# Attention kernel: one score product split in 128 and 384 columns in half of the phases, and 160 wait instructions a batch between projection products

## Chip, cores, metric

The kernel runs on one core of one Trainium2 chip. The metric is device time in microseconds of one execution, the median of three runs. An engine is named as in the profile: PE is TensorE's matmuls, PEld its weight loads, DVE is VectorE, ACT is ScalarE, POOL is GpSimd, SP is SyncE.

## What is computed

The input x is (32, 256, 32, 32) in f32: 32 batches, 256 channels, 1024 tokens. Each group of 8 channels is normalised over its 8 x 1024 values. From the result q, k and v are projected (256 to 256 each), there are 8 heads of 32 channels, and a strictly causal attention over the 1024 tokens follows; x is added.

```python
x = x + conv_attention(_gn(x), q_w, q_b, kv_w, kv_b)
# in it, by head:
scores = einsum('bhqd,bhkd->bhqk', q, k) / sqrt(32)
scores = where(mask == 0, -10000.0, scores)      # mask: tril(ones, -1)
attn   = where(mask == 0, 0.0, softmax(scores))
out    = einsum('bhqk,bhkd->bhqd', attn, v)
```

## The kernel before

All is f32. A batch is worked through in two halves, one for each group g of four heads (128 channels). Each half has six phases, numbered i = 0 to 5, the entries of the list VISITS; so there are twelve phases a batch, v = 0 to 11, and 32 x 12 in all. The text calls a phase by its i.

**A phase** has four steps on TensorE, and the main loop at the end of `unshifted` writes them down in this order by hand; nothing is reordered later, since the whole body stands in a manual schedule.

1. `scores(b, v)`: the transposed scores of one or two blocks of keys against their queries, as products of 32 rows (a head's channels) by 64 columns of keys. Each entry of VISITS is made once for each of four heads and two halves of the keys. "Long" entries are up to 512 queries wide; their results go into two tiles, `pairs[0]` for heads 0, 1 and `pairs[1]` for heads 2, 3. "Short" entries, among them the diagonal pairs (built by `pair`: one product of 128 and one of 64 columns for each half of the keys), go into `pairs[2]`.[...]
2. the units that fall due at this phase (`at`): one unit of projection for a later phase or batch. `projections(b)` makes twelve of them, `project_qk` eight times (two input halves cc, each four products of 512 columns by `product`, L169) and `project_v` four times (four groups of four products of 256 columns).
3. `values(b, v - 1)`: exponentials of the phase ahead times v (L422), 12 or 16 products.
4. what stands in `between` and `after`: the small products of the norm of a later batch (pm, pv, L169), sums, and the transfers.

ScalarE takes the exponentials of each phase out of PSUM, `pairs[0]`, `pairs[1]` (L397) and then `pairs[2]` (L393), and evicts projections and values. GpSimd masks the diagonals (L339) and issues the adding transfers of key sums, VectorE adds exponentials over keys for the softmax sums and finishes outputs, SP issues loads and stores.

**The order inside `scores`.** It starts with the short entries of heads 2, 3 (`short_of((2, 3))`), then the long ones of heads 0, 1 (`begin`), then the first long one of heads 2, 3. Then TensorE waits until the short entries of heads 2, 3 are finished (semaphore `bank_free`[...]), and the short ones of heads 0, 1 follow. Phases 0, 1, 3 and 4 are in PAIRS, which tells that their short entry is a diagonal pair. Where such a phase has a second long entry (phase 0 alone), its product of heads 0, 1 is put between the two parts of the diagonal pair of heads 2, 3, which then run in reverse order, 64 columns first. Phases 1, 3 and 4 have one long entry, 512 columns wide.

`live["arrived"]` is a semaphore that ScalarE raises to 1 when the first part of x has come, at the very start, and to 2 a little later. SP waits on it in two places; so does GpSimd, 64 times in a row, ahead of its first work (L669).

Of the kernel before, what the change touches and what calls it, by code (L numbers as in the profile page):

```python
# [17 lines left out]
P = 128  # L18
HD = 32
CPG = 8  # L20
HALF = 512
# [11 lines left out]
def tile_norm_attention_residual(  # L33
# [19 lines left out]
    nc = tc.nc  # L53
    B, C, H, W = x.shape
    S = H * W
    NG = C // P
# [42 lines left out]
    def unshifted():  # L99
        live = {}  # L100
# [56 lines left out]
        def spare(name):  # L157

            live["turn"] = live.get("turn", -1) + 1
            if live["turn"] in (1, 3, 5):  # L160
                return ps_o.tile([P, HALF], F32, tag="acc", name=name)
            return misc(name)
# [68 lines left out]
        def norm_apply(b, hf, g):  # L231
# [5 lines left out]
            for s in range(2):  # L237
# [5 lines left out]
                else:  # L243
                    nc.scalar.activation(to, of, AF.Identity, bias=live["shift", b][:, g : g + 1], scale=rstd)  # L244

        def project_qk(b, g, n, hf):

            key = ("qk"[n], b, g)
            if hf == 0:
                live[key] = qkpool.tile([P, S], F32, tag="qk"[n], name=f"{'qk'[n]}_{b}_{g}")  # L250
            cols = slice(hf * HALF, (hf + 1) * HALF)
            pp = spare(f"pp_{b}_{g}_{n}_{hf}")
            for cc in range(NG):
                product(
                    pp, wT[:, cc, n * C + g * P : n * C + (g + 1) * P], live["xn", b, hf][:, cc, :],
                    start=cc == 0, stop=cc == NG - 1,
                )
            nc.scalar.activation(
                live[key][:, cols], pp, AF.Identity, bias=qk_bias[:, n, g : g + 1], scale=(SCALE, 1.0)[n],
            )  # L260

        def project_v(b, n):


            if n == 0:
                live["v", b] = work.tile([P, NB, C], F32, tag="v", name=f"v_{b}")
            pp = spare(f"ppv_{b}_{n}").rearrange("p (s c) -> p s c", c=C)
            hf, at = divmod(2 * n * P, HALF)
            for s in range(2):
                tokens = slice(at + s * P, at + (s + 1) * P)  # L270
                for cc in range(NG):
                    product(
                        pp[:, s, :], live["xn", b, hf][:, cc, tokens], wT[:, cc, 2 * C : 3 * C], start=cc == 0, stop=cc == NG - 1,
                    )
            nc.scalar.copy(live["v", b][:, 2 * n : 2 * n + 2, :], pp)  # L275

        def projections(b):
# [29 lines left out]
        def score(b, g, bank, j, op):  # L307

            c, kb, first, width, cols = op
            rows = slice(HD * j, HD * (j + 1))  # L310
            return nc.tensor.matmul(  # L311
                bank[c : c + KEYS, cols], lhsT=live["k", b, g][rows, kb * P + c : kb * P + c + KEYS],
                rhs=live["q", b, g][rows, first : first + width], start=True, stop=True, skip_group_check=True,
            )

        def scores_of(b, g, bank_of, heads, entries, between=lambda: None, order=slice(None)):
# [9 lines left out]
                                done.setdefault((j, c), []).append(score(b, g, bank_of(j), j, ops[n]))  # L326
            return done

        def mask(b, g, raw, j):


            hf, place = j // 2, (2 * j % 4) * P
            if ("e", b, g, "D", hf) not in live:
                live["e", b, g, "D", hf] = epool.tile(
                    [P, 4, HALF], F32, tag=("e0", "e")[hf], bufs=4, name=f"diagonal_{b}_{g}_{hf}"
                )
            square = live["e", b, g, "D", hf]
            for s in range(2):
                nc.gpsimd.affine_select(  # L339
                    out=square[:, :, place + s * P : place + (s + 1) * P],  # L340
                    in_=raw[:, :, (1 - s) * KEYS : (3 - s) * KEYS],
                    pattern=[[0, 4], [(1, -1)[s], P]], compare_op=ALU.is_gt, fill=0.0, base=0,
                    channel_multiplier=(-1, 1)[s],
                )
            if j == 0:
                nc.gpsimd.memset(square[0:1, :, 0:1], 1.0)

        def scores(b, v):


            g, i = divmod(v, len(VISITS))
            longs, shorts = VISITS[i]
            name = f"{b}_{g}_{i}"
            e = epool.tile([P, 4, HALF], F32, tag="e0" if i == TOTAL else "e", bufs=4, name=f"e_{name}")
            eh = epool.tile([P, 4, HALFBANK], F32, tag="eh", bufs=3, name=f"eh_{name}")
            pairs = [ps_s.tile([P, 2, HALF], F32, tag="sT", name=f"sT_{name}_{a}") for a in range(3)]
            short = pairs[2].rearrange("p bank (n q) -> p bank n q", n=2)
            short_of = lambda heads, *how: scores_of(
                b, g, lambda j: short[:, j % 2, j // 2, :], heads, shorts, *how
            )  # L360
            long_of = lambda heads, n: scores_of(b, g, lambda j: pairs[j // 2][:, j % 2, :], heads, longs[n : n + 1])
            rest = [lambda: long_of((2, 3), 1)] if len(longs) > 1 else []
            begin = [lambda n=n: long_of((0, 1), n) for n in range(len(longs) - 1, -1, -1)]
            if i in PAIRS and len(longs) > 1:
                first = short_of((2, 3), begin.pop(0), slice(None, None, -1))
            else:
                first = short_of((2, 3))
            for f in begin:
                f()
            long_of((2, 3), 0)  # L370

            ends = [made[-1] for made in first.values()]
            first = [ins for made in first.values() for ins in made]
            for ins in ends:
                ins.then_inc(bank_free, 1)
            for ins in first:
                tc.no_tile_sem_insts.add(ins.ins.name)
            live["free"] = live.get("free", 0) + len(ends)
            wait = nc.tensor.wait_ge(bank_free, live["free"])
            for ins in first:  # L380
                tc.declare_no_dep(wait.ins, ins.ins, reason="the semaphore orders them")
            made = short_of((0, 1), *rest if i in PAIRS else ())
            if i not in PAIRS:
                for f in rest:
                    f()
            for made in made.values():
                for lo in made:
                    for ins in first:
                        tc.declare_no_dep(lo.ins, ins.ins, reason="the semaphore orders them")
            wide, narrow = (max(at + width for at, width, _ in entries) for entries in (longs, shorts))  # L390
            for a in range(3):
                if a == 2:
                    exp = nc.scalar.activation(  # L393
                        eh.rearrange("p (n bank) q -> p bank n q", n=2)[:, :, :, :narrow], short[:, :, :, :narrow], AF.Exp
                    )
                else:
                    nc.scalar.activation(e[:, 2 * a : 2 * a + 2, :wide], pairs[a][:, :, :wide], AF.Exp)  # L397

            for ins in first:
                tc.add_to_no_dep_group(f"first_{name}", ins.ins)  # L400
                tc.add_to_no_dep_group("first", ins.ins)
            tc.declare_no_dep(exp.ins, group=f"first_{name}", reason="through the last two products")
            tc.declare_fence(exp.ins, group=f"first_{name}")
            live["e", b, g, "L", i], live["e", b, g, "H", i] = e, eh
            if i in PAIRS:
                mask(b, g, eh, PAIRS[i])

# [182 lines left out]
        ]  # L590
        N, TOTAL = NG * len(VISITS), 2
        PAIRS = {0: 0, 1: 1, 3: 3, 4: 2}

        PRODUCTS = [
            (0, [
# [36 lines left out]
        at, between, after = {}, {}, {}  # L632
# [22 lines left out]
        SPREAD = (2, 2, 4, 5)  # L655
        FINISH = (N + 13, N + 13, N + 14, N + 16)
        every = range(4)
        ALIGN = 24, 64

        with tc.manual_schedule(engines={ENG.PE, ENG.Activation, ENG.DVE, ENG.Pool, ENG.SP}):  # L660
# [4 lines left out]
            load_weights(junk)  # L665
            for _ in range(ALIGN[0]):
                nc.vector.drain()
            for _ in range(ALIGN[1]):
                nc.gpsimd.wait_ge(live["arrived"], 1)  # L669
# [36 lines left out]
            for b in range(B):  # L706
                first, last = b * N, b == B - 1
# [3 lines left out]
                if b >= 2:  # L711
                    for n in range(NG * NH):
                        cols = slice(n % NH * HALF, (n % NH + 1) * HALF)
                        v = max(first - 2 * N + LOAD, 0)
# [4 lines left out]
                if not last:  # L719
                    for n in every:  # L720
                        v = first + SUMS[n]
# [5 lines left out]
                    v = first + N + (5 if late else 6)  # L727
# [8 lines left out]
                    for n in every:  # L736
                        v = first + (N + 9 + n // 2 if late else FINISH[n])
# [12 lines left out]
            for i in range(B * N + 1):  # L750
# [4 lines left out]
                b, v = divmod(i - 1, N)  # L755
# [23 lines left out]
    def shifted():  # L779


        with ExitStack() as inner:
# [34 lines left out]
            with tc.For_i(0, B, 1) as b:  # L817
# [93 lines left out]
                )  # L911

    inside = unshifted()
    ALL = 3 * P * ROW
    held = nc.values_load(
# [29 lines left out]
```

## Time and profile before

| what | value |
|---|---|
| median of three runs | 1793.78 us (1793.7 to 1794.42) |
| the profiled execution | 1793.44 us, its span 1791.7 us |
| mean granted TensorE clock | 0.999 |
| one batch, first projection to first projection | 55.09 us |
| products of the program on TensorE; matmuls in the profile | 18,568; 37,036 |
| TensorE busy at scores, values, q/k projections, v projections | 578.4, 401.0 and 158.7, 492.2, 247.5 us |

How to read it: a matmul of f32 runs as two passes, so the profile has two matmuls and two weight loads for one product of the program. [...]the distance between the starts of groups of four is what a group takes. The ends of matmuls are modelled. Where a text gives starts in ns, they are those of single instructions in the trace, counted from the first score product of the phase.

### The profile page before, as it was taken

What the parts mean: (1) busy time and instruction counts of PE and PEld (TensorE: products, weight loads), DVE (VectorE), ACT (ScalarE), POOL (GpSimd) and SP (SyncE); (2) the same over time, 40 slices, a digit from 0 to 9 for tenths busy, and PEclk for the clock granted to TensorE, in tenths of its full rate; (3) what the DMA queues carried; (4) which work ended last, traced back from release to release, by engine and by line L of the source; (5) the groups of instructions that cost most, each with busy time, mean ns of one, the idle gap of its engine ahead of it and who ended that gap; (6) DMA issues with size and microseconds to landing.
All of it is one profiled execution on the core that took longest, in us unless ns stands there. A gap on an engine that the chain in (4) does not pass through costs nothing.

```text
span 1791.7 us, 81825 instructions
## 1 busy us (share of the span) xinstructions
PE 1784.4 (100%) x37036; PEld 948.2 (53%) x37036; DVE 1673.4 (93%) x1826; ACT 1456.4 (81%) x1990; POOL 881.3 (49%) x903
## 2 busy tenths in 40 slices
PE   9999999999999999999999999999999999999998
PEld 5555555555555555555555555555555555555554
DVE  4689999999999999999999999999999999999998
ACT  6888878888788888788887888878888878888785
POOL 2345544554545555445554455454555544555452
PEclk9999999999999999999999999999999999999999
DMA  2566766767667766766676676767776667666664
GB/s 70 105 115 137 134 134 129 147 135 143 127 126 149 140 138 134 135 139 138 139 135 131 129 150 132 145 125 128 149 141 135 136 134 138 139 139 137 132 107 106
DMA packets 86818, 236.77 MB, mean 132 GB/s; under 512 B 21312, under 2 KB 22336, under 8 KB 70592
## 3 DMA queue, kind: packets, MB, share of 16 engines
q0 software_dynamic: 15872, 97.53, 40.1%
q1 hardware_dynamic: 70448, 133.89, 25.5%
q8 instruction: 290, 4.75, 1.1%
q14 instruction: 64, 0.52, 0.1%
q10 hardware_dynamic: 144, 0.07, 0.0%
HBM read 66.85 MB, written 34.57 MB: 57 GB/s over the span
## 4 chain that ended last, share of the span: by engine, by line
PE 99%; ACT 0%; DVE 0%; issue 0%; POOL 0%; POOLq 0%
PE sT L311 31%; PE acc L422 28%; PE pp L169 26%; PE ppv L169 13%; PE pd L474 1%; PE busy L155 0%; ACT e L397 0%; PE pv L169 0%; PE pm L169 0%; PE wt L148 0%; DVE rb_last L547 0%; ACT eh L393 0%; DVE rb_last L534 0%; DVE turned L531 0%; DVE acc L544 0%
## 5 line engine op out<-in xcount | busy, mean ns | idle before, releaser
L339 POOL TENSOR_SCALAR_AFFINE_SELECT diagonal<-eh 128x512 f32<-128x512 f32 x512 | 632.5, 1256 | 841.5 <-ACT eh L393 840.9
L397 ACT ACTIVATE e<-sT 128x1024 f32<-128x1024 f32 x768 | 744.4, 1022 | 250.3 <-PE sT L311 225.9
L440 DVE TENSOR_TENSOR e<-e,e 128x1024 f32<-128x1024 f32 x314 | 574.2, 1829 | 24.5 <-ACT v L275 3.2
L311 PE MATMUL sT<-q,k 32*64 32x128 f32 (+2 forms) x18432 | 578.4, 372 | 0.1
L311 PEld LDWEIGHTS sT<-q,k 32*64 32x64 f32 x18432 | 394.8, 131 | 188.4 <-PE sT L311 69.6
L169 PE MATMUL pp<-xn,wT 128*32 128x512 f32 x4096 | 492.2, 598 | 0.0
L422 PE MATMUL acc<-e,v 128*32 128x512 f32 (+3 forms) x4608 | 401.0, 450 | 0.0
L393 ACT ACTIVATE eh<-sT 128x768 f32<-128x768 f32 (+1 forms) x384 | 341.7, 890 | 0.0
L422 PEld LDWEIGHTS acc<-e,v 128*32 128x32 f32 x4608 | 149.2, 110 | 261.5 <-issue 238.9
L169 PE MATMUL ppv<-wT,xn 128*32 128x256 f32 x4096 | 247.5, 382 | 0.0
L440 DVE TENSOR_TENSOR diagonal<-diagonal,e 128x1536 f32<-128x1536 f32 x126 | 195.0, 1548 | 16.8 <-PE acc L422 9.2
L169 PEld LDWEIGHTS pp<-xn,wT 128*32 128x32 f32 x4096 | 107.0, 109 | 195.7 <-issue 163.7
L440 DVE TENSOR_TENSOR e<-e,eh 128x1024 f32<-128x1024 f32 x126 | 164.2, 1303 | 6.5
L422 PEld LDWEIGHTS acc<-diagonal,v 128*32 128x32 f32 x4096 | 121.1, 110 | 87.6 <-issue 76.0
L440 DVE TENSOR_TENSOR e<-e,diagonal 128x2048 f32<-128x2048 f32 x63 | 144.2, 2289 | 19.8 <-POOL diagonal L339 19.8
L169 PEld LDWEIGHTS ppv<-wT,xn 128*32 128x32 f32 x4096 | 120.1, 109 | 79.7 <-issue 7.0
L422 PE MATMUL acc<-diagonal,v 128*32 128x128 f32 x4096 | 158.7, 273 | 0.0
L244 ACT ACTIVATE xn<-x,shift,rstd 128x256 f32<-128x256 f32 x248 | 136.8, 608 | 0.6 <-POOL shift L229 0.6
L544 DVE TENSOR_TENSOR num<-num,rb 128x512 f32<-128x512 f32 x124 | 123.3, 994 | 0.2 <-DMA rb<-inverses 0.2
L453 POOL DMA_DIRECT2D e<-e x124 | 103.3, 833 | 38.2 <-issue 38.2
L547 DVE SCALAR_TENSOR_TENSOR rb<-num,v_bias_col,x 128x256 f32<-128x256 f32 x248 | 117.5, 515 | 4.4
L453 POOL DMA_DIRECT2D diagonal<-diagonal x124 | 104.1, 839 | 4.8 <-issue 4.8
(84 smaller groups left out, 984.4 us busy)
## 6 DMA issues: line engine op xcount, KB each, us to landing
x<-in_x_dram SPq DMA_DIRECT2D x124, 256.0 KB, 3.7
diagonal<-diagonal POOLq DMA_DIRECT2D x62, 512.0 KB, 5.4
e<-e POOLq DMA_DIRECT2D x62, 512.0 KB, 5.9
rb<-inverses SPq DMA_DIRECT2D x124, 256.0 KB, 3.9
out_dram<-rb SPq DMA_DIRECT2D x124, 256.0 KB, 4.9
diagonal<-diagonal POOLq DMA_DIRECT2D x62, 256.0 KB, 4.6
folded<-diagonal SPq DMA_DIRECT2D x62, 256.0 KB, 5.1
e<-e POOLq DMA_DIRECT2D x62, 256.0 KB, 5.0
```

What stands on the lines that cost most here:

```text
L169: nc.tensor.matmul(out[part], lhsT=lhsT[:, part], rhs=rhs, start=start, stop=stop, skip_group_check=True)
L244: nc.scalar.activation(to, of, AF.Identity, bias=live["shift", b][:, g : g + 1], scale=rstd)
L311: return nc.tensor.matmul(bank[c : c + KEYS, cols], lhsT=live["k", b, g][rows, kb * P + c : kb * P + c + KEYS], rhs=live["q", b, g][rows, ...
L339: nc.gpsimd.affine_select(out=square[:, :, place + s * P : place + (s + 1) * P], in_=raw[:, :, (1 - s) * KEYS : (3 - s) * KEYS], pattern=[ ...
L393: exp = nc.scalar.activation(eh.rearrange("p (n bank) q -> p bank n q", n=2)[:, :, :, :narrow], short[:, :, :, :narrow], AF.Exp)
L397: nc.scalar.activation(e[:, 2 * a : 2 * a + 2, :wide], pairs[a][:, :, :wide], AF.Exp)
L422: nc.tensor.matmul(acc[HD * j : HD * (j + 1), of], lhsT=live["v", b][:, kb, h * HD : (h + 1) * HD], rhs=e[:, j, :], start=first, stop=last ...
L440: nc.vector.tensor_add(to, to, tile_of(b, g, at))
L453: nc.gpsimd.dma_start(out=total[:rows], in_=total[rows : 2 * rows], accum_op=ALU.add)
L474: nc.tensor.matmul(pd[HD * j : HD * (j + 1), of], lhsT=pick, rhs=e[:, j, :], start=start, stop=stop, skip_group_check=True,)
L544: nc.vector.tensor_mul(num, num, rb)
L547: nc.vector.scalar_tensor_tensor(blocks(rb, s), blocks(num, s, (start + s) % 2 == 1), v_bias_col[:, g : g + 1], blocks(xt[:, g, cols], s), ...
```

## The change

- `part_of` is new: it issues the one long entry of a phase for heads 0, 1 and for a slice of its columns. In `scores`, for the phases in SPLIT (v = 1, 3, 4, 7, 9, 10, which are i = 1, 3, 4 of both halves of a batch), `begin` becomes two pieces, the first 128 columns and the other 384. Since `begin` now has two pieces there, these phases also take the branch that only phase 0 took: the 64-column parts of the diagonal pair of heads 2, 3 come first, then the 128-column piece of heads 0, 1, then the 128-column parts of heads 2, 3, then the 384-column piece. The long product of heads 2, 3 stays whole.
- `fill` is new: n times TensorE waits for `arrived` to be at least 1. It is called after each group of four products of the projections, with the counts in FILL: 14 and 12 in a `project_qk`, 8, 8, 6, 6 in a `project_v`. In the built program two such waits share one instruction: 5120 wait instructions are added, 160 a batch, and 768 products.

```diff
+        def fill(n):
+
+            for _ in range(n):
+                nc.tensor.wait_ge(live["arrived"], 1)
+
         def project_qk(b, g, n, hf):
...
                     start=cc == 0, stop=cc == NG - 1,
                 )
+                fill(FILL[0][cc])
...
                         pp[:, s, :], live["xn", b, hf][:, cc, tokens], wT[:, cc, 2 * C : 3 * C], start=cc == 0, stop=cc == NG - 1,
                     )
+                    fill(FILL[1][NG * s + cc])
...
+        def part_of(b, g, bank, entry, of):
+
+            at, _, halves = entry
+            for j in (0, 1):
+                for ((c, kb, first, _, cols),) in halves:
+                    score(b, g, bank[:, j, :], j, (
+                        c, kb, first + of.start, of.stop - of.start, slice(cols.start + of.start, cols.start + of.stop)
+                    ))
...
             begin = [lambda n=n: long_of((0, 1), n) for n in range(len(longs) - 1, -1, -1)]
-            if i in PAIRS and len(longs) > 1:
+            if v in SPLIT:
+                begin = [lambda n=n: part_of(b, g, pairs[0], longs[0], n) for n in (slice(0, P), slice(P, HALF))]
+            if i in PAIRS and len(begin) > 1:
                 first = short_of((2, 3), begin.pop(0), slice(None, None, -1))
...
         PAIRS = {0: 0, 1: 1, 3: 3, 4: 2}
+        SPLIT = 1, 3, 4, 7, 9, 10
...
         every = range(4)
+        FILL = (14, 12), (8, 8, 6, 6)
         ALIGN = 24, 64
```

## The prediction

> **What bounds the kernel now.** I read the page first: the busy table, then the chain that ended last.
>
> ```profile
> PE 1784.4 (100%) x37036; PEld 948.2 (53%) x37036; DVE 1673.4 (93%) x1826; ACT 1456.4 (81%) x1990; POOL 881.3 (49%) x903
> ...
> PE 99%; ACT 0%; DVE 0%; issue 0%; POOL 0%; POOLq 0%
> PE sT L311 31%; PE acc L422 28%; PE pp L169 26%; PE ppv L169 13%; PE pd L474 1%; PE busy L155 0%; ACT e L397 0%; PE pv L169 0%; PE pm L169 0%; PE wt L148 0%; DVE rb_last L547 0%; ACT eh L393 0%; DVE rb_last L534 0%; DVE turned L531 0%; DVE acc L544 0%
> ```
>
> TensorE is never without work, and the chain is its own: scores (L311), values (L422), projections (L169). A saving counts in full, as long as no other engine comes late. Then the chain in order of time:
>
> ```profile
> 98.32 1.88 PE pp L169 x16
> 125.82 1.89 PE ppv L169 x32
> 153.41 1.88 PE pp L169 x16
> ```
>
> The same projection comes 55.09 us later (153.41 - 98.32): one batch, and it repeats so for all of them. Last, the six phases of the first half of a batch, each as a window from its first score product to the next projection (phases 0, 1, 2, 3, 4, and 5 of the half ahead; columns: window, length, busy time and instructions of PE and PEld at L311, clock, share of the DMA engines, GB/s):
>
> ```profile
> 431.97:433.39 1.42, 1.42 (x64) 1.16 (x64) 1.00 0.51 185
> 436.54:437.94 1.40, 1.40 (x48) 1.06 (x48) 1.00 0.09 18
> 441.10:442.57 1.47, 1.47 (x32) 0.80 (x32) 1.00 0.90 89
> 445.30:446.70 1.40, 1.40 (x48) 1.05 (x48) 1.00 0.96 152
> 450.29:451.69 1.40, 1.40 (x48) 1.05 (x48) 1.00 0.02 1
> 427.34:428.82 1.48, 1.48 (x48) 1.03 (x48) 1.00 0.66 230
> ```
>
> Phases 1, 3, 4 take 1.40 us (single starts: 1404 ns; it is 1403 to 1411 in all batches). Phase 0, which already has a long product of heads 0, 1 in 128 and 384 columns, takes 1.42 (1419 ns). So splitting as such is no gain; the order inside a phase must be followed.
>
> [...] Here it is 91 to 94 ns from the end of the last score column to the first projection.
>
> **The split.** Starts in ns from the start of the phase, the first of each group of four (heads x key halves), both passes:
>
> ```
> phase 0 now   heads 2,3: 64 @0,106    128 @165,276  384 @386,708   128 @1031,1140
>               heads 0,1: 128 @26,186  384 @296,618  128 @941,1050   64 @1159,1215   next @1419
> phase 1 now   heads 2,3: 128 @0,160   64 @269,325   512 @383,815
>               heads 0,1: 512 @53,534  128 @963,1073  64 @1182,1238                  next @1404
> ```
>
> The two head pairs are two chains side by side, and the longer one sets the end. In phase 1 it is that of heads 0, 1: it begins 53 ns late and then has no gap. After the change, phases 1, 3, 4 issue 64 (2,3), 128 (0,1), 128 (2,3), 384 (0,1), 512 (2,3), then 128 and 64 (0,1). That is phase 0's order in the first five groups, with 512 for 384, and without its last 128 of heads 2, 3. So I take phase 0's starts:
>
> - heads 0, 1: 128 @26,186; 384 @296,618; 128 @941,1050; 64 @1159,1215. The fourth of the last group starts 20 later, at 1235, and its columns end at 1235 + 53 = 1288.
> - heads 2, 3: 64 @0,106; 128 @165,276; 512 @386. In phase 0 the second to fourth product of this group load their weights at 355, 371, 388 and not beside the first, at 278. These are products 18 to 20 of the phase; 355 is 32 ns after the first product's end (323)[...]. The changed phase has as many ahead of them, so the delay stays: the fourth streams from 388 + 53 = 441, its second pass from 870, and ends at 870 + 429 = 1299.
>
> The later end is 1299; with 93 for the drain the projection starts at 1392. Now it is 1403.5: 11.5 ns a phase less. Six phases a batch, 32 batches: 192 x 11.5 = **2.2 us less**. Entering a phase costs the same (202 ns after a 128-column value product in phase 0 as in phase 3).[...]
>
> Bounds: without the delayed loads heads 0, 1 decide, 1288 + 93 = 1381, 22.5 less, -4.3 us. If the end is ragged as in phase 0 (1419), 15.5 more, +3.0 us.
>
> **The waits.** fill asks for 14 + 12 in each of eight q/k units and 28 in each of four v units, 320 a batch; the built program has two conditions in one instruction, so 160 instructions a batch, 5120 in all. They stand on TensorE's own queue; behind them are the products of the same unit, then the values. "arrived" is at 1 from the start, so none blocks. What they take is issue time, e each. The only rows:
>
> ```profile
> L169 PEldq EVENT_SEMAPHORE  x67: 51/51/51, 7.2 to 1693.0; - x67
> ```
> ```profile
> L669 POOLq EVENT_SEMAPHORE  x32: 42/43/43, 4.3 to 7.0; - x32
> ```
>
> TensorE's own are 51 ns each, and the products around them keep their 429 ns, so they are taken ahead of the array. GpSimd's 32, in a row and of the same kind, lie 87 ns apart (2.7 us / 31). I take 51 and keep 87 as the upper end. Does issue fall behind? In a changed phase the first projection products have entered by about 1170 (products 12 to 15 end at 1099 to 1119, plus 32 and four times 16.5, the pace of the late loads). A v unit then needs 14 waits and three more groups of 66 ns: the values enter at 1170 + 14e + 198. TensorE asks for them at 1392 + 240 + 7 x 216 = 3144. At e = 51 that is 2082, 1.06 us early; at 87, 2586; it is late only above e = 127. A q/k unit: 1170 + 13e + 66 against 1392 + 453 + 3 x 429 = 3132, late above 145. So the waits cost 0, hidden by the products of their own unit. Before the first scores, TensorE waits for xn and evictions anyway, and 7 waits (357 ns) lie beside 858 ns of products; 0.
>
> **Instruction fetch.** Queue 8 brings TensorE's instructions: 4.75 MB in 290 packets, one for 256 of 74,150 instructions. A batch has 2306 now, nine packets; then 2306 + 24 x 4 + 160 = 2562, ten. No phase differs between batches although the packets' places shift by 2 instructions a batch, so a packet costs nothing now; I take 0.
>
> **Others.** ScalarE's first exponential of a phase starts 1208 ns in, and 1185 in phase 0, so about 23 ns earlier; heads 2, 3 end up to 55 later, but their exponential waits behind the first (1022 ns). Ahead of phase 3 ScalarE's last one ends only 162 ns ahead of the next phase; it moves along with TensorE. No DMA is added or moved; SP's wait for bank_free is met at the same time (128's end at 276 + 268 = 544, now 64's end at 325 + 217 = 542).
>
> Sum: 0 - 2.2 + 0. The profiled execution took 1793.44 (span 1791.7, 1.7 around it), so 1791.2; the median of the runs is 0.34 above it: **1791.6 us**.
>
> **The rivals.**
> - The forecast, 1791.6 (1790.3 to 1793.0). Chance 0.52.
> - The loads are not late[...]: -4.3, 1789.5. For it: phase 1 now shows no late load. Against: the same 16 products are ahead. 0.20.
> - The end is ragged as in phase 0, +3.0: 1796.8. For it: phase 0 measures 1419. Against: its last products are late behind a 128 of heads 2, 3 that the changed phases lack. 0.12.
> - Slower by the waits: with two conditions a wait takes longer than 51. From e = 127 on the values of v units come late. At 131 (1.5 x 87) it is 14 x 131 + 1368 - 3144 = 58 ns in each of 128 units, 7.4 us: 1793.8 - 2.2 + 7.4 = 1799.0. For it: no such instruction is on this queue now. Against: 87 on GpSimd. 0.09.
> - Ten packets in the time of nine: one a batch comes 0.2 us too late, +6.4, 1798.0. Against: issue is over a microsecond ahead. 0.07.
> - That the change does not do what it says is excluded: the built program has 18,568 + 768 products and the 5120 waits.
>
> **How the numbers follow.** About 0.2% (3.6 us) can be told from no change. Forecast, ragged end and a little of the second rival are inside it, 0.62; faster 0.20, the second rival; slower 0.18, the last two and a ragged end that is somewhat worse. The range takes in the first three cases (0.84): 1788.5 to 1797.5.
>
> **What would show it.** Right: phases 1, 3, 4 at about 1392 ns, batches at 55.09 - 0.07 = 55.02 us, late loads at 355 to 388 for the 512 of heads 2, 3, phases 0, 2, 5 as now, projections with 429 and 216 ns between groups. Wrong: gaps in front of values or inside projections (waits), phases that differ from batch to batch (fetch), or 1381 or 1419 for the changed phases.

## The result and the profile after

| | us, median | runs |
|---|---|---|
| before | 1793.74 | 1793.43 to 1794.42 |
| after | 1853.72 | 1844.38 to 1860.76 |

The ratio is 1.0332, with a 95% interval of 1.0298 to 1.0367: 60 us slower, where 2 us faster was forecast. The runs of the kernel after also lie 16 us apart, those of before 1 us. The profiled execution took 1856.89 us, its span 1855.1.

From the page of the kernel after, the busy table and the chain that ended last:

```profile
PE 1809.7 (98%) x38572; PEld 968.1 (52%) x38572; DVE 1655.7 (89%) x1826; ACT 1453.9 (78%) x1990; POOL 817.7 (44%) x903
...
PE 97%; issue 2%; ACT 1%; DVE 0%; DMA 0%; POOLq 0%; POOL 0%; SPq 0%; ACTq 0%
PE sT L318 30%; PE acc L440 28%; PE pp L169 26%; PE ppv L169 13%; PE pd L492 1%; ACT e L415 0%; DMA x<-in_x_dram 0%; PE pm L169 0%; ACT eh L411 0%; PE pv L169 0%; PE wt L148 0%; ACT v L282 0%; POOLq L689 0%; DVE rb_last L565 0%; DVE rb_last L552 0%
```

TensorE is still its own chain, but 2% of the span is "issue": time in which it waited for nothing that the profile shows. That was 0% before. The six phases as windows of the scores (L318), in batch 7 (columns as before: window, length, busy time and instructions of PE and PEld, clock, DMA share, GB/s), phases 0 to 5:

```profile
414.12:415.54 1.42, 1.42 (x64) 1.16 (x64) 1.00 0.98 190
418.69:420.08 1.39, 1.39 (x56) 1.09 (x56) 1.00 0.02 6
423.23:424.71 1.48, 1.48 (x32) 0.80 (x32) 1.00 0.30 33
427.43:428.82 1.39, 1.39 (x56) 1.09 (x56) 1.00 0.96 183
432.68:434.06 1.38, 1.38 (x56) 1.09 (x56) 1.00 0.04 12
437.26:438.74 1.48, 1.48 (x48) 1.02 (x48) 1.00 0.80 282
```

The scores are shorter, as forecast: 1387 to 1388 ns in phases 1, 3, 4 by single starts. So the loss is elsewhere. The view of waits, TensorE's issue rows (us in total, times, longest), before and then after:

```profile
PEld acc L422 <- issue: 315.0, 1144, 0.4
...
PEld ppv L169 <- issue: 7.0, 34, 0.3
```
```profile
PEld acc L440 <- issue: 347.9, 1147, 2.7
...
PEld ppv L169 <- issue: 14.3, 39, 2.6
```

In before a weight load idles ahead of values 1144 times, with the products themselves busy for 1784.4 of the span's 1791.7 us, but never for more than 0.4 us. Now there are idle times of 2.7 us. The same view for the products themselves, where before has no row of issue:

```profile
PE acc L440 <- issue: 26.3, 22, 2.3
PE ppv L169 <- issue: 5.1, 4, 2.1
...
PE sT L318 <- issue: 2.4, 5, 1.2
```

Next I took the distance between the first score products of consecutive phases, less the same distance in before (where it is equal in all batches), over batches 1 to 30, by phase of the batch v (0 to 11). An ordinary table, worked out from the starts in the trace:

```
v             0     1    2     3     4    5    6    7    8     9    10   11    sum
excess, us  0.0   7.3  0.0  24.7  -0.6  0.0  0.3  0.5  0.0  30.3  -0.2  0.0   62.3
```

Three phases hold it all, and not in each batch: one v = 9 loses 4.2 us, another none. The batch, always 55.09 us before, now takes between 54.98 and 60.58. There are 46 places where a product starts over 150 ns later than it should; they sum to 45.7 us, and the rest of the 62 is made of smaller delays in the groups right behind them. **36 of the 46, with 42.7 us, begin at one and the same kind of place**: the executed TensorE instruction number 256k + 449 (counted from 0), which is the first one of packet k of the instruction queue (322 packets for the 82,345 TensorE instructions in the trace, one for 256). The queues on the pages of before and after (packets, MB, share of 16 engines):

```profile
q0 software_dynamic: 15872, 97.53, 40.1%
q1 hardware_dynamic: 70448, 133.89, 25.5%
q8 instruction: 290, 4.75, 1.1%
```
```profile
q0 software_dynamic: 15872, 97.53, 37.3%
q1 hardware_dynamic: 70448, 133.89, 25.5%
q8 instruction: 322, 5.28, 1.2%
```

Here is one such stall, v = 3 of batch 3, in the timeline of the kernel after (start, us, engine, line):

```profile
230.92 1.47 PE L440 MATMUL acc<-e,v 128*32 128x512 f32 x14
233.82 0.38 PE L440 MATMUL acc<-e,v 128*32 128x256 f32 x1 [1.43 <-issue]
```
```profile
231.78 0.12 PEld L440 LDWEIGHTS acc<-e,v 128*32 128x32 f32 x3 [0.30 <-issue]
233.82 0.11 PEld L440 LDWEIGHTS acc<-e,v 128*32 128x32 f32 x1 [1.92 <-issue]
```

Fourteen passes of a group of sixteen run, three of four weight loads, and then nothing for 1.43 us, in the middle of a group whose inputs are all there. The matmul at 233.82 is the first instruction of packet 38. TensorE reached packet 37 at 226.82; the fetch of 38 began only at 231.11 and landed at 232.35; TensorE went on 1.47 us later. The windows around it, after and then in the variant "light_adds" below (columns: window, length, busy of PE, PEld, DVE, ACT, POOL, clock, DMA share, GB/s):

```profile
224.00:228.00 4.00, 4.00 (x92) 1.80 (x81) 3.86 (x7) 4.00 (x7) 1.85 (x3) 1.00 0.82 175
228.00:232.00 4.00, 4.00 (x100) 2.33 (x90) 3.79 (x7) 4.00 (x8) 0.27 (x1) 1.00 0.91 177
232.00:236.00 4.00, 2.57 (x70) 1.38 (x65) 4.00 (x3) 1.15 (x4) 2.93 (x2) 1.00 0.25 74
```
```profile
224.00:228.00 4.00, 4.00 (x112) 2.58 (x108) 3.83 (x8) 3.70 (x6) 0.00 (x0) 1.00 0.35 95
228.00:232.00 4.00, 4.00 (x96) 2.16 (x92) 3.86 (x5) 3.12 (x6) 2.78 (x2) 1.00 0.24 45
```

The packet is late while the DMA engines are 82% and 91% busy. At 35% (light_adds) packet 38 begins 0.39 us after TensorE reached packet 37, not 4.3. The trace of before shows the same relation: where the DMA engines were over 90% busy in the 1.5 us after TensorE reached the packet ahead (118 packets), the fetch began a median of 1.8 us after that moment; where they were under 10% busy (41 packets), it began right at it. Over the whole runs ("slack" is from the landing of a packet to the start of its first instruction on TensorE; "begin" is from TensorE reaching the packet ahead to the beginning of the fetch):

```
                slack, ns                      begin, us         a packet's 256
            min    median   below 1600     median    max         take, median us
before     1604    4334     0 of 277        0.67     3.93        6.04
after      1214    2924    62 of 309        1.30     5.35        5.34
```

In after, all 37 packets at whose first instruction TensorE had started nothing for over 0.3 us have a slack of 1.2 to 1.6 us, so that is how soon it resumes after a landing. Before, the least was 1604: no stall, and nothing to spare.

### The profile page after: what moved, and what is told of

The parts are those of the page before. It is cut to its first block, busy times and chain, and to the rows that moved or that the text cites. A ratio compares the mean times of both kernels' runs of the same rounds, so it can differ in the third digit from the quotient of the medians.

```text
span 1855.1 us, 90017 instructions
## 1 busy us (share of the span) xinstructions
PE 1809.7 (98%) x38572; PEld 968.1 (52%) x38572; DVE 1655.7 (89%) x1826; ACT 1453.9 (78%) x1990; POOL 817.7 (44%) x903
## 4 chain that ended last, share of the span: by engine, by line
PE 97%; issue 2%; ACT 1%; DVE 0%; DMA 0%; POOLq 0%; POOL 0%; SPq 0%; ACTq 0%
PE sT L318 30%; PE acc L440 28%; PE pp L169 26%; PE ppv L169 13%; PE pd L492 1%; ACT e L415 0%; DMA x<-in_x_dram 0%; PE pm L169 0%; ACT eh L411 0%; PE pv L169 0%; PE wt L148 0%; ACT v L282 0%; POOLq L689 0%; DVE rb_last L565 0%; DVE rb_last L552 0%
## 5 line engine op out<-in xcount | busy, mean ns | idle before, releaser
L355 POOL TENSOR_SCALAR_AFFINE_SELECT diagonal<-eh 128x512 f32<-128x512 f32 x512 | 548.2, 1091 | 969.1 <-ACT eh L411 969.1
L318 PE MATMUL sT<-q,k 32*64 32x128 f32 (+2 forms) x19968 | 581.0, 357 | 2.8 <-issue 2.4
L458 DVE TENSOR_TENSOR e<-e,e 128x1024 f32<-128x1024 f32 x314 | 551.8, 1757 | 31.9 <-PE acc L440 7.5
L318 PEld LDWEIGHTS sT<-q,k 32*64 32x64 f32 x19968 | 402.2, 131 | 183.6 <-PE sT L318 61.5
L440 PE MATMUL acc<-e,v 128*32 128x512 f32 (+3 forms) x4608 | 417.5, 454 | 27.7 <-issue 25.1
L440 PEld LDWEIGHTS acc<-e,v 128*32 128x32 f32 x4608 | 153.4, 110 | 297.6 <-issue 270.4
L458 DVE TENSOR_TENSOR e<-e,eh 128x1024 f32<-128x1024 f32 x126 | 170.3, 1352 | 6.5
L565 DVE SCALAR_TENSOR_TENSOR rb<-num,v_bias_col,x 128x256 f32<-128x256 f32 x248 | 123.8, 539 | 4.4
L562 DVE TENSOR_TENSOR num<-num,rb 128x512 f32<-128x512 f32 x124 | 117.8, 950 | 0.1
L458 DVE TENSOR_TENSOR e<-e 128x512 f32<-128x512 f32 x64 | 52.7, 824 | 67.8 <-PE acc L440 58.8
```

The lines of the kernel that those rows point to most:

```text
L318: return nc.tensor.matmul(bank[c : c + KEYS, cols], lhsT=live["k", b, g][rows, kb * P + c : kb * P + c + KEYS], rhs=live["q", b, g][rows, ...
L355: nc.gpsimd.affine_select(out=square[:, :, place + s * P : place + (s + 1) * P], in_=raw[:, :, (1 - s) * KEYS : (3 - s) * KEYS], pattern=[ ...
L440: nc.tensor.matmul(acc[HD * j : HD * (j + 1), of], lhsT=live["v", b][:, kb, h * HD : (h + 1) * HD], rhs=e[:, j, :], start=first, stop=last ...
L458: nc.vector.tensor_add(to, to, tile_of(b, g, at))
L562: nc.vector.tensor_mul(num, num, rb)
L565: nc.vector.scalar_tensor_tensor(blocks(rb, s), blocks(num, s, (start + s) % 2 == 1), v_bias_col[:, g : g + 1], blocks(xt[:, g, cols], s), ...
```

## Experiments

The theory: one packet is fetched ahead (in before a fetch begins from 1.5 us before to 3.9 us after TensorE reaches the packet ahead of it, in after from 0.9 before to 5.35 after, first and last 60 us left out); with more instructions a batch, and instructions that take issue time, the fetches at the DMA-loaded places come too late (theory "fetch"). The rivals: the waits themselves hold TensorE back ("issue"), or the order of the scores does it ("split"). The forecasts ahead of the runs name theories by letters: W and I say that the issue time of the waits does it; P and N, that the number and the place of the packets do, whatever fills them; L, that packets land late because the DMA engines are busy. Each run was made beside runs of the kernel before on the same chip, 1793.4 to 1793.7 us; ratios are to those.

**split_only**: the split, no waits (2402 TensorE instructions a batch; after has 2562, before 2306).

```diff
-        FILL = (14, 12), (8, 8, 6, 6)
+        FILL = (0, 0), (0, 0, 0, 0)
```

> The split with no wait instruction (FILL all 0): 2402 instructions a batch, so the places of the instruction packets drift by 98 a batch. Theory W (the waits: 106 ns of issue each hold TensorE's queue back, so that packets are asked for late and no lead is left to hide one that comes late): no stalls, the split's 16.5 ns in 192 phases alone, 1793.7 - 3.2 = 1790.5 us. Theory P (more than nine packets a batch, at places where a short block meets busy DMA engines, stall, whatever fills them): stalls in those batches in which a packet falls on such a place, 1796 to 1815 us.

Measured: 1800.82 us, 1.0038 (1.0026 to 1.0051). The changed phases take 1387 ns as in after. But v = 10 loses 4.2 us and v = 1 loses 3.9 in the profiled run; 8 of its 12 gaps are at packet starts, and its least slack is 1211 ns. So the split gains, and even its 96 instructions a batch (2402 is no multiple of 256, so packets drift over all places) give back more than the gain.

**waits_only**: the waits, no split (2466 a batch).

```diff
-        SPLIT = 1, 3, 4, 7, 9, 10
+        SPLIT = ()
```

> The waits with no split (SPLIT empty): 2466 instructions a batch. Theory W: stalls at about the rate of the full change, 1835 to 1860 us, issue idle in front of single products all along. Theory P: drifting places, stalls in some batches only, 1800 to 1825 us. If waits alone cost by their issue time and not through packets, gaps come in every unit of v at the same place, and the time is the same in every batch.

Measured: 1827.72 us, 1.0189 (1.0151 to 1.0227), between the two forecasts. The excess (31.1 us) is spread over v = 0, 1, 3, 5, 9 and 10, with the drift of the packets. The longest wait for issue is now at a projection:

```profile
PEld pp L169 <- issue: 162.8, 520, 2.5
```

Waits alone cost 34 us and the split alone 7; together 60, so they aren't a sum of two separate costs. The packets lie elsewhere in each of the three, though, so this doesn't part number from place.

**shift_half**: the full change and one more wait instruction behind each group in batches 1 to 4, 128 in all: half a packet, so that from batch 5 on all packets begin elsewhere.

```diff
-                fill(FILL[0][cc])
+                fill(FILL[0][cc] + 2 * (0 < b < 5))
...
-                    fill(FILL[1][NG * s + cc])
+                    fill(FILL[1][NG * s + cc] + 2 * (0 < b < 5))
```

> The full change with two waits more after each group of projection products in batches 1 to 4, 128 instructions in all, so that from batch 5 on every packet lies half a packet away from where it lay. Theory W: the place does not matter, 1845 to 1862 us. Theory P: another place, other stalls, at other phases: under 1825 or over 1875 us.

Measured: 1838.77 us, 1.024 (1.0219 to 1.026), again between the forecasts. In the profiled run (1850.49 us, the longest of the four) the stalls left v = 3 and 9 and went to v = 0 (26.2 us), 10 (9.9), 5 (8.6) and 11 (4.9), with the same waits in the same places of the later batches. This speaks for the fetch and against "issue" as the whole: the waits are the same, and what moved is where packets begin.

**order_only**: the kernel before, with the 64-column parts first in all phases of PAIRS, but the 512 columns of heads 0, 1 whole: the new order, no instruction more.

```diff
-            if i in PAIRS and len(longs) > 1:
+            if i in PAIRS:
```

> The kernel before with the order of phase 0 in phases 1, 3, 4 but the long product of heads 0, 1 whole (64-column parts first, then 512, then 128): no instruction more, no wait. Both theories: no stalls, since count and places of instructions stay. By the starts of the phases, heads 0, 1 begin at 26 and not at 53[...]: a changed phase takes 1377 and not 1403.5, 192 x 26.5 = 5.1 us less, 1788.6 us.

Measured: 1883.68 us, 1.0504 (1.0486 to 1.0521), far off what was expected, and with another cause. Windows of phases 0, 1 and 3 of batch 7 (scores, L311), and phase 1 in the timeline:

```profile
423.81:425.23 1.42, 1.42 (x64) 1.16 (x64) 1.00 0.82 202
428.38:430.25 1.87, 1.87 (x48) 0.97 (x48) 1.00 0.00 0
...
437.60:439.46 1.86, 1.86 (x48) 0.96 (x48) 1.00 0.46 141
```
```profile
429.75 0.42 PEld L311 LDWEIGHTS sT<-q,k 32*64 32x64 f32 x16 [0.83 <-PE sT L311]
```

The last short products of heads 0, 1 wait 0.83 us and start at 1373 ns instead of 963. They wait for `bank_free`, raised by the short products of heads 2, 3; with those behind the 512 columns of heads 0, 1 in program order, the semaphore came only after these had ended: their last ends at 527 + 587 = 1114 ns by its modelled end, and the four raises come at 1200 to 1328 ns, in after at 558 to 686. So it is the 128-column piece that makes the order usable: in after the load that waits for the semaphore starts at 727 ns, here at 1371.

**light_adds**: the full change, but the adding transfers of GpSimd move two rows of key sums in place of 64 or 32, which leaves out most of these sums.

```diff
-            nc.gpsimd.dma_start(out=total[:rows], in_=total[rows : 2 * rows], accum_op=ALU.add)
+            nc.gpsimd.dma_start(out=total[:2], in_=total[rows : rows + 2], accum_op=ALU.add)
```

> The full change, but each of the adding transfers of key sums on GpSimd's queue moves two rows and not 64 or 32, so most of that queue's 97.5 MB is left out; TensorE's instructions are the same in number and place. It leaves out part of the sums over keys. Theory L (packets land late because the DMA engines are busy): the time from asking to landing falls, stalls go to nearly none, 1790 to 1800 us. Rival (a packet takes its time whatever else moves, and the issue is too fast for it): stalls stay, 1840 to 1860 us.

Measured: **1790.59 us, 0.9983 (0.9976 to 0.9989)**. All TensorE instructions and waits are as in after. The page's queues and the view of waits:

```profile
q1 hardware_dynamic: 70448, 133.89, 26.5%
q0 software_dynamic: 7936, 4.11, 2.1%
q8 instruction: 322, 5.28, 1.3%
```
```profile
PEld acc L440 <- issue: 314.9, 1144, 0.4
```

No stall is left (0.4 us again), the least slack is 2025 ns, the fetch begins at most 2.36 us late, and the wait instructions still stand 106 ns apart. So neither the waits nor the split delay TensorE here, where no packet comes late. **before_light**, the same edit in the kernel before, tells what the lighter transfers are worth by themselves:

> The kernel before with the adding transfers of key sums cut to two rows, which leaves out part of the sums over keys. Both theories: no stall is there to be saved, so the time stays, 1793.0 to 1793.8 us. If the lighter traffic speeds TensorE in another way, it is lower by about what the full change gained from it.

Measured: 1793.68 us, 1.0001 (0.9993 to 1.001): nothing. So what light_adds gains, 2.9 us by the medians beside it and 3.0 in batches 1 to 30 of its profile, is the split's alone.

**raises**: 160 semaphore raises a batch in place of the waits: the same number of instructions. **raises_half** has in addition 32 more in each of batches 1 to 4, half a packet.

```diff
-                nc.tensor.wait_ge(live["arrived"], 1)
+                nc.tensor.sem_inc(live["counted"], 1)
...
-        FILL = (14, 12), (8, 8, 6, 6)
+        FILL = (7, 6), (4, 4, 3, 3)
```

> The full change with its 160 wait instructions a batch replaced by 160 instructions that raise a semaphore nobody waits for: the same number, the same places, another issue time than the 106 ns measured for a wait with two conditions. Theory W (issue time of the waits takes the lead away): if a raise takes about half or less, few stalls, 1791 to 1810 us. Theory P (the number of instructions in the time of a batch, at these places): as the full change, 1840 to 1860 us.

> As with the raising instructions, and one more after each group of projection products in batches 1 to 4, 128 in all, so that packets lie half a packet away from batch 5 on. Theory W: the place matters little, the same as without the shift within 10 us. Theory P: the stalls lie elsewhere and their sum is another, 15 us or more away from it.

Measured: 1922.31 us (1.0738, 1.0699 to 1.0778) and 1926.27 (1.0769, 1.0718 to 1.0819); both theories had expected less for the first. A raise takes 150 ns of issue. The prediction's own sum would then have the values of a v unit late by 1368 + 14 x 150 - 3144 = 324 ns, 128 times, and those of a q/k unit by about 54, 256 times: 55 us. The traces show less of this. The units of v stand in v = 3, 4, 9 and 11, and in phases with no late packet the first three of these are late by some 113 ns and the last by 20, two of the eight q/k units by 36 and the rest by nearly nothing: about 14 us. The rest is stalls again. Excess by phase, as above, of raises and then of raises_half:

```
v             0     1    2     3     4    5    6    7    8     9    10   11    sum
raises      2.3   1.1  0.0  31.3   4.9  0.1  1.5  0.8  0.0  59.3   3.6  1.5  106.3
raises_half 56.8  3.5  0.1   7.4   7.0  5.1  5.7  2.0  0.1   6.2   6.3 13.0  113.2
```

In raises, 42 of the 46 gaps over 0.6 us (first and last 60 us left out) are at packet starts, and the loss lies in v = 3 and 9 as in after. Half a packet further it lies in v = 0, as in shift_half. So the place decides where it stalls; and with the same number of instructions at the same places, 44 ns more of issue each make the loss about twice that of after, with 14 of its 129 us by direct lateness.

**split_two**: the split in v = 3 and 9 alone, no waits (2338 a batch).

```diff
-        SPLIT = 1, 3, 4, 7, 9, 10
+        SPLIT = 3, 9
...
-        FILL = (14, 12), (8, 8, 6, 6)
+        FILL = (0, 0), (0, 0, 0, 0)
```

> The split in phase 3 of both halves alone, no waits: 2338 instructions a batch. 64 phases of 16.5 ns are 1.1 us. Theory P and W alike: with 32 instructions a batch more than before packets come nearly as rarely as before; their places drift by 34 a batch over all places in eight batches. No stall: 1792.6; with stalls at the places that stalled with the whole split: up to 1796 us.

Measured: 1800.17 us, 1.0042 (1.0027 to 1.0056), above the highest forecast. It stalls at v = 1 (4.0 us) and v = 10 (3.2), which it doesn't change. Thirty-two instructions a batch suffice, since they carry packets into places where before none begins.

**few_waits**: the kernel before and 12 wait instructions a batch (2318).

```diff
-        SPLIT = 1, 3, 4, 7, 9, 10
+        SPLIT = ()
...
-        FILL = (14, 12), (8, 8, 6, 6)
+        FILL = (2, 0), (2, 0, 0, 0)
```

> The kernel before, no split, with one wait instruction in each projection unit: 12 a batch, 1.3 us of issue time a batch, 2318 instructions, so that the places of packets drift by 14 a batch instead of 2. Theory I: 1793.6, no more. Theory N, in the form that the place alone can stall (a block of dense instructions meeting busy DMA engines): stalls in the batches where the places are bad, 1795 to 1802 us.

Measured: 1798.23 us, 1.0029 (1.0019 to 1.0039), 4.4 of 5.3 us of excess at v = 1; four of its six gaps are at packet starts. One wait instruction in a unit is little as issue time (106 ns of over a microsecond of lead). What it changes is the drift: 14 instructions a batch past nine packets, in place of 2, so that packets come to begin at v = 1.

**half_waits**: the split and 76 wait instructions a batch (2478).

```diff
-        FILL = (14, 12), (8, 8, 6, 6)
+        FILL = (7, 6), (4, 4, 3, 3)
```

> The split with half the waits (76 instructions a batch, 0.7 us of issue time a unit instead of 1.4). Split alone took 1800.8, the full change 1853.7. Theory I: the lead is still over half a microsecond, stalls near those of the split alone, 1800 to 1810 us. Theory N: about half way, 1820 to 1835 us.

Measured: 1814.91 us, 1.0129 (1.0095 to 1.0164), between the forecasts. With fewer than half of the waits the loss is about a third of after's: it grows faster than their number, but the packets drift here too, so place has its part in this.

**tiny_products**: the split, and in place of the waits 40 products of two columns a batch: 160 instructions that are no waits and take some of TensorE's own time (in before the two passes of such products, pm and pv, start 28 ns apart).

```diff
+            product(pp[:, :2], wT[:, 0, n * C + g * P : n * C + (g + 1) * P], live["xn", b, hf][:, 0, :2])
...
+            if n < 2:
+                product(pp[:, 0, :2], live["xn", b, hf][:, 0, at : at + P], wT[:, 0, 2 * C : 2 * C + 2])
...
-        FILL = (14, 12), (8, 8, 6, 6)
+        FILL = (0, 0), (0, 0, 0, 0)
```

> The split, and in place of the 160 waits a batch 40 products of 2 columns, four ahead of ten of the twelve projection units: again 160 instructions a batch (2562, the same places), but issued at the pace of products and not at 106 ns each. The units overwrite what they give. They take TensorE's time: two passes of about 27 ns for four of them, 10 x 55 ns x 32 = 17.6 us. Theory I (it is the issue time of the waits that takes the lead): few stalls, 1808 to 1818 us. Theory N (it is ten packets in the time of nine at these places): the full change's stalls, 1845 to 1875 us.

Measured: 1830.26 us, 1.0207 (1.0189 to 1.0224). That is between the forecasts. In phases without a stall the four products ahead of a unit take 63 to 64 ns; less the split's gain that is 15.9 us in 30 batches, 16.9 in 32. The rest, 1830.26 - 1793.38 - 16.9 = 20.0 by the medians, 15.5 by the phases of the profiled run (13.1 of it at v = 1), is stall. With the same number of instructions a batch, the waits of after lose 63 (60 and the split's 3). So some 43 to 47 of these 63 us go with the waits and 16 to 20 with the number and place of instructions. This is not a clean division: the stalls lie at v = 1 and not at 3 and 9, so the places are not those of after, and a batch is longer by the products' own time.

**loads, loads_q, loads_h, loads_t**: 160 unused 16-bit weight loads a batch in place of the waits, and 64, 128 and 192 more in the first batches, to place the same number of packets at four places. They should part number from place in those 16 to 20 us.

```diff
-                nc.tensor.wait_ge(live["arrived"], 1)
+                nc.tensor.ldweights(pick.bitcast(mybir.dt.bfloat16)[:, :HD])
```

> The split, and in place of the 160 waits a batch 160 weight loads that nothing uses (32 columns, 16-bit): again 2562 instructions a batch, at the places of the full change, with no wait, and beside the products. Theory number (ten packets in the time of nine cannot all be in time): what the run with products of 2 columns had left after their own time, 16 to 22 us, 1806 to 1813 us. Theory place (which instructions stand ahead of a packet when the DMA engines are busy): at this place the same 1806 to 1813, but other places differ by 8 us or more. If the loads hold the array up[...], it is over 1830.

> As with the 160 weight loads, and one more after each group in batches 1 and 2, 64 instructions, a quarter of a packet later from batch 3 on. Theory number: within 5 us of the first. Theory place: another sum of stalls; a good place gives 1791 to 1795 us, below the kernel before at best.

> The same, half a packet later (128 instructions, batches 1 to 4). Theory number: within 5 us of the first. Theory place: another sum again, 1791 to 1825 us.

> The same, three quarters of a packet later (192 instructions, batches 1 to 6). Theory number: within 5 us of the first. Theory place: another sum again, 1791 to 1825 us.

Measured: 2112.18 (1.1774, 1.1755 to 1.1794), 2113.02 (1.1779, 1.1759 to 1.1798), 2121.89 (1.1827, 1.1807 to 1.1847) and 2125.29 us (1.1853, 1.1833 to 1.1872). The means failed: these loads stopped the array. From the list of groups and the timeline of "loads":

```profile
L249 PEld LDWEIGHTS <-pick 128*32 128x32 bf16 x5120 | 169.0, 93 | 640.2 <-issue 640.2
```
```profile
502.21 2.80 PE L169 MATMUL ppv<-wT,xn 128*32 128x256 f32 x32
```

A v unit takes 2.80 us in place of 1.73; all units together lose some 320 us over the program. TensorE then has less to do per unit of time and the fetch more time to come. The 8 to 13 us by which loads_h and loads_t are longer than loads are about what 128 and 192 more such loads take at 62 ns each (the 299.5 us of excess in 30 batches over 4800 loads). Nothing follows on the place.

## Why the prediction was wrong

- **Split, mechanism right, size somewhat off.** The order of starts came out as written: 64 at 0, 107; 128 at 165, 277; 512 at 386, 815, with late loads at 354, 371, 388 and second passes up to 870; heads 0, 1 at 27, 187, 296, 618, 941, 1050, 1159, 1215, last 1235. The end of the columns, 1299, is right. The term that was off is the time from there to the first projection, which the prediction calls the drain: 93 was taken from phase 1, 88 to 89 is measured here, so 1387.5 and not 1392: -16 ns, 192 times, -3.1 us in place of -2.2. light_adds shows 2.9. The starts rest on what one pass of an f32 product takes in the trace of before: 109 ns at 128 columns, 429 at 512; 53 for 64 columns is an estimate from these two (320 ns for 384 columns), and the same 53 lies between the last late load and its product's first pass (870 - 429 - 388). The first pass of phase 1 takes 160 ns there, the later ones of 128 columns 109 to 110. The four products of a group run at the same time: those of a q/k group of before start at 0, 7, 14 and 20 ns, with records of 617 ns each, and the next four at 454 to 474. What holds the late loads back isn't shown; they came late behind 16 products in phase 0 of before and again here. The rivals "loads not late" and "ragged end" are excluded by the same starts.
- **Waits: "What they take is issue time, e each. ... I take 51 and keep 87."** Measured: the records are 51 each, but they begin 106 ns apart, 13 of them in 1.30 to 1.34 us and 14 in 1.49. The record that the estimate was read from:

```profile
L249 PEldq EVENT_SEMAPHORE  x5120: 51/51/51, 10.9 to 1824.1; - x197
```

  The record is not the whole price: 55 of the 106 ns are outside it. These waits were met and raise nothing, so what fills the 55 is not shown. The sum's own first term, an estimate, is near: in phase 1 of batch 7 the first wait behind the first four projection products begins at 1157 ns, where the sum lets these products enter by 1170. 106 is below 127, so by the prediction's own sum the values aren't late, and light_adds confirms that. At 150 (raises) they are, by 113 ns and not by the 324 of that sum, which puts the limit nearer 142 than 127 (113 over 14 instructions is 8 ns each). But it was wrong to put "the waits cost 0": they use up the lead. By the same sum the values of a v unit enter at 1368 + 14 x 106 = 2852, 0.29 us before they are wanted, where without waits it was 1.78. That lead had a second user.
- **Instruction fetch, the step that failed: "No phase differs between batches although the packets' places shift by 2 instructions a batch, so a packet costs nothing now; I take 0."** The observation was true and the conclusion too wide. 2306 is 9 x 256 + 2: the packets shift by 62 instructions in all, a quarter of a packet, so the kernel before had tried only a quarter of the places. And the slack of its worst packet was 1604 ns, where in after TensorE resumes up to 1.6 us after a landing. The quarter of the places and the 1604 could be read from the trace of before; that 1604 is the very edge could not, since nothing stalls there. In after, 2562 is 10 x 256 + 2, so the bad places (packets 1, 3 and 8 of ten) come back each batch; a packet's time fell to 5.34 us; and the lead that would have covered a late packet was used by the waits. The rival "ten packets in the time of nine" named the resource, but priced it as one shortfall of 0.2 us a batch, 6.4 us; it was about 2 us a batch. Its argument against, that issue is over a microsecond ahead, is the lead that the waits used. The sign that the prediction gave for the fetch, phases that differ from batch to batch, is what came.
- **What is shown, and what isn't.** That TensorE stands at packet starts, that this goes away with the load on the DMA engines (light_adds), that it moves with the packets (shift_half, raises_half, few_waits, split_two) and that issue time makes it worse (raises against after, same number and places) are shown. That a fetch begins late because it stands behind other transfers on the DMA engines is argued from the windows, from light_adds and from the delays of before at high and low load; the order inside an engine isn't in the trace. How the loss parts into number, place and issue time is open: tiny_products changed the places too, the raises issue more slowly, and the loads stopped the array. A version with the adding transfers moved in time or made smaller without leaving anything out wasn't tried. No version here that computes the whole beats the kernel before; the split is worth about 3 us, and only where the fetch has room.

## What to carry to other kernels

Where one engine's instructions run without a gap, count them as a resource with a supply: packets of 256 here, each fetched about one ahead, and in before a median of 1.8 us later where the DMA engines were over 90% busy than where they were under 10%. Look in the trace at the least slack between a packet's landing and its first instruction before adding any (1604 ns in before, 1214 in after). Here instructions that blocked nothing still used up the lead of issue (14 waits of 106 ns are 1.48 us of 1.78), and a longer issue at the same places (raises, 150 ns in place of 106) made late packets dearer: 129 us in place of 60. The price of a wait was its distance to the next one, 106 ns, not its record of 51. And if equal batches show no stall, ask how many of the possible alignments they have tried.

## What the hardware showed that I had not expected

- A met wait with two conditions held TensorE's queue for 106 ns (after), though its record shows 51; a raise of a semaphore held it for 150 (raises).
- In after a fetch of 256 TensorE instructions took about 1.0 us, but began up to 5.35 us after TensorE had reached the packet ahead (4.3 us in the stall shown, with the DMA engines 82% to 91% busy); where TensorE stood at a packet's first instruction, it went on 1.2 to 1.6 us after the landing.
- Products of the two head pairs started out of program order (in after, the 128 columns of heads 0, 1 start at 27 ns, before the second pass of the 64 of heads 2, 3 at 107), but in order_only a semaphore raised by short products came at 1200 ns, after the end (1114) of the 512 columns ahead of them in the program, where it came at 558 in after: +0.46 us a phase.
- 16-bit weight loads between f32 products stopped the array (loads): about 0.4 us between the last f32 load and the first of them, some 10 us a batch.
